# Four-layer graph attention on one core: the third step becomes a one-head step, and the small columns W·a of layers 1 to 3 are built by TensorE

## The chip, the core and the metric

The kernel runs on one core of one Trainium2 chip. The engines named below are TensorE (PE, with its weight loads as PEld), VectorE (DVE), ScalarE (ACT), GpSimd (POOL) and SyncE (SP), which issues nearly all DMAs. The metric is device time of one execution in microseconds. All arithmetic is float32, and the masks are stored as bytes.

## The reference

Sixteen graphs of 1024 nodes with 256 features pass through four graph-attention layers that share one adjacency matrix. Layers 0 and 2 have four heads of 64 features, layers 1 and 3 one head of 256. Each layer normalises its input, projects it, forms attention weights from two inner products per node and head, takes a masked softmax over the neighbours, aggregates, applies an activation and adds the result to x. Cut to what is computed:

```python
h = jnp.maximum(_layernorm(x, axis=-1), 0.0)
q = (h @ W).reshape(B, N, H, D)
e_src = jnp.einsum('bnhd,d->bnh', q, a_src)
e_dst = jnp.einsum('bnhd,d->bnh', q, a_dst)
e = e_src[:, :, None, :] + e_dst[:, None, :, :]
e = jnp.where(e >= 0, e, ALPHA * e)
e = jnp.where(mask, e, NEG_INF)
attn = jax.nn.softmax(e, axis=2)
x = x + jax.nn.elu(jnp.einsum('bijh,bjhd->bihd', attn, q))   # relu in layer 3
```

## The kernel before, in words

One step is one layer of one graph: 64 steps, numbered from 0. Four graphs are in flight at a time (`STREAMS`), and `order_of_steps` (L699) interleaves them. With H for a four-head step and 1 for a one-head step, the order starts H H H 1 H 1 1 H 1 H 1 and alternates from there on. Step 0 is graph 0 in layer 0, step 1 graph 1 in layer 0, step 2 graph 2 in layer 0, step 3 graph 0 in layer 1, step 4 graph 3 in layer 0, steps 5 and 6 graphs 1 and 2 in layer 1, step 7 graph 0 in layer 2.

**The weights.** A softmax weight is, up to a factor that cancels, max(G, r)·mask, where G is one row broadcast to all 128 partitions and r a column. For each head there are eight tiles w of 128 x 1024 (L411), one DVE instruction each. A four-head step thus has 32 tiles, a one-head step 8. The tiles live in a pool "w" of 18 slots (`WBUFS`). The pool also takes the small tensors of `weight_columns`. A slot is free again when the last reader of its tile has run.

**The aggregation.** A step has eight groups of matmuls (L428), each closed by an ACT copy of the result y (L443). In a four-head step two groups use the eight tiles of one head. A group goes through its four row blocks one after another, and each block needs all eight tiles, so only the first quarter of a group can run while the last tile is being made. In a one-head step each group is one row block of all eight tiles.

**The preparation of a step** (`preparation`, L231) has 21 pieces: statistics of x on DVE (L243), their combination (L263 to L284, mostly on POOL), normalisation on ACT (L290), the transpose of both halves of the rows, projection on PE (L332) with ACT copies (L334), the column factors (L340 to L351), and the row G. In most steps the transpose is done by two ACT copies and one DMA (L299, L301, L307), and the row G by a PE transpose, a write to DRAM and a read that broadcasts it (L358, L362, L386), which ACT copies into PSUM (L397). Steps 0 and 1 and the last step transpose on PE (L321). Steps 0 and 63 also build their G on PE (L394).

**The end of a step** (`finish`, L449) divides by the softmax sums, applies the activation and adds to x. It is shared between DVE, POOL and ACT. The third step from the end has a form of its own (L504 to L533) in which DVE does nearly all of it, since the last step needs its result at once.

**The order.** It is written out by hand, and each engine runs its instructions in program order. Position 8n + k is group k of step n. Each piece of the preparation of step n has a due position, from one of the tuples `FOUR`, `ONE`, `SOON` and so on, plus a start. At each position the loop (L673 to L694) emits in this order: end pieces of the step before that are due before the group, the tiles that the group needs, the group, further end pieces, row copies G, a piece of `later` (below), due preparation, and then tiles in advance, at most 18 beyond the last head that is done. A step's tiles can be emitted only after its last preparation piece.

**W·a.** Two columns per head of the weights are W·a, so that the projection yields the inner products too. `weight_columns` (L136) computes them by layer in four pieces: fetch a as one row (one DMA, L145), spread it over the partitions by a matmul and an ACT copy (L152, L155), eight DVE operations and a square (L162, L163, L169), and a bound for the exponents (L175 to L182). For layers 1, 2 and 3 the dictionary `later` puts these pieces at positions p, p + 1, p + 2 and p + 8 with p = 1, 27 and 43.

Of the kernel before, what the change touches and what calls it, by code (L numbers as in the profile page):

```python
# [26 lines left out]
F32 = mybir.dt.float32  # L27
# [20 lines left out]

FOUR = (-8, -8, -5, 0, 1, 0, 3, 5, 5, 5, 5, 1, 4, 5, 5, 5, 5, 6, 8, 8, 10)
SHORT = (-4, -4, -4, 0, 1, 0, 3, 5, 5, 5, 5, 1, 4, 5, 5, 5, 5, 6, 8, 8, 10)
NEXT = (-4, -4, -4, 1, 3, 2, 5, 8, 8, 8, 8, 4, 7, 8, 8, 8, 8, 9, 10, 10, 12)
ONE = (2, 2, 2, 3, 4, 3, 5, 7, 7, 7, 7, 4, 7, 8, 8, 8, 8, 8, 11, 11, 12)
SOON = (0, 0, 0, 1, 2, 1, 3, 4, 4, 5, 5, 2, 5, 6, 6, 7, 7, 7, 8, 8, 10)
FIRST = (-4, -4, -4, -2, -0.9, -1, -1, -0.8, -0.8, -0.8, -0.8, 0, 0, 1, 1, 1, 1, 1, 2, 2, 4)
TIGHT = (4, 4, 4, 5, 6, 5, 7, 8, 8, 8, 8, 6, 8, 9, 9, 9, 9, 9, 10, 10, 12)
LAST = (0, 0, 0, 1, 3, 2.8, 2.8, 4, 4, 4, 4, 4, 4, 4, 4, 4, 4, 4, 5, 5, 5)
LATE = (0, 0, 0, 1, 2, 1, 3, 4, 4, 4, 4, 2, 4, 5, 5, 5, 5, 5, 6, 6, 8)

# [10 lines left out]
def kernel(ctx: ExitStack, tc: tile.TileContext, x, adj, ws, avs, out):  # L71
# [41 lines left out]
    xs = {}  # L113
    state = [dict() for _ in steps]

    def bank(*shape):
        t = ps.tile([P, 512], F32, name="bank")
        n = math.prod(shape)
        if len(shape) == 1:
            return t[:, 0:n]  # L120
        names = "abc"[:len(shape)]
        return t[:, 0:n].rearrange(f"p ({' '.join(names)}) -> p {' '.join(names)}",
                                   **dict(zip(names, shape)))
# [10 lines left out]
                            in_=ws[l][k * P:(k + 1) * P, :].rearrange("p (h d) -> p h d", h=H))  # L134

    def weight_columns(l):  # L136

        H, slope, hs, _ = LAYERS[l]
        D = F // H
        st = {}  # L140

        def vectors(queue=nc.sync):

            st["a"] = work.tile([P, HALF, H, D], F32, name="w", bufs=WBUFS)
            queue.dma_start(  # L145
                out=st["a"][0:1, 2:4],
                in_=bass.AP(tensor=avs[l].tensor, offset=avs[l].offset,
                            ap=[[0, 1], [D, 2], [hs, H], [1, D]]))

        def spread():  # L150
            pa = bank(2, H, D)
            nc.tensor.matmul(pa.rearrange("p t h d -> p (t h d)"), lhsT=ones[0:1, :],  # L152
                             rhs=st["a"][0:1, 2:4].rearrange("p t h d -> p (t h d)"),
                             start=True, stop=True)
            nc.scalar.activation(st["a"][:, 0:2], pa, AF.Copy)  # L155

        def columns(ks=range(K)):
            for k in ks:
                for part in range(2):
                    prod = st["a"][:, 2 + part]  # L160
                    wk = heads_of(wx[l], H)[:, k]
                    nc.vector.tensor_mul(prod, wk[:, :, 0:D], st["a"][:, part])  # L162
                    nc.vector.tensor_reduce(  # L163
                        wk[:, :, D] if part else wx[l][:, k, F + H:F + 2 * H], prod, AX.X, ALU.add)
            if K - 1 not in ks:
                return
            st["sq"] = small.tile([P, K, H], F32, name="sq", bufs=1)
            wd = heads_of(wx[l], H)[:, :, :, D]
            nc.vector.tensor_tensor(st["sq"], wd, wd, op=ALU.mult)  # L169

        def bound():

            pn = bank(H)
            for k in range(K):
                nc.tensor.matmul(pn, lhsT=ones, rhs=st["sq"][:, k, :], start=(k == 0),  # L175
                                 stop=(k == K - 1))
            top = small.tile([P, 1], F32, name="top", bufs=1)
            nc.vector.tensor_reduce(top, pn, AX.X, ALU.max)
            nc.gpsimd.tensor_tensor(top, top, half1, op=ALU.pow)
            nc.gpsimd.tensor_scalar(cbias[l], top, 16.01, None, op0=ALU.mult)  # L180
            nc.gpsimd.tensor_scalar(nbias[l], top, -16.01 * slope, None, op0=ALU.mult)
            nc.gpsimd.tensor_scalar(rbias[l], top, -16.01 * (1.0 - slope), SHIFT,  # L182
                                    op0=ALU.mult, op1=ALU.add)

        return vectors, spread, columns, bound

    pairs = {}
# [43 lines left out]
    def preparation(n):  # L231
# [6 lines left out]
        def stats(half):  # L238
            if half == 0:
                st["bn"] = small.tile([P, C, 6], F32, name="bn")  # L240
            bn = st["bn"]
            for c in range(half * HALF, (half + 1) * HALF):
                nc.vector.bn_stats(bn[:, c, :], xs[b][:, c, :])  # L243
            q = slice(half * HALF, (half + 1) * HALF)
            if n == len(steps) - 1:
                combine(q, nc.vector)
            elif n == 0:
                if half == 1:
                    combine_end(slice(0, HALF), nc.vector)
                combine(q, nc.vector)  # L250
            elif H == 1:

                combine(q, nc.gpsimd)
                combine_end(q, nc.gpsimd)
# [55 lines left out]
                st["turned", half].rearrange("p s n i -> p (n i) s"), AF.Copy)  # L310

        def transpose(half, k):
            if 1 < n < len(steps) - 1:

                (merge if k else split)(half)
                return
            if k == 0:
                st["hT", half] = prep.tile([P, K, HALF * P], F32, name="rows", bufs=HBUFS)
            pt = bank(HALF, P)
            for q in range(HALF):  # L320
                nc.tensor.transpose(pt[:, q, :], st["xn", half][:, k, q, :], ident)  # L321
            nc.scalar.activation(st["hT", half][:, k, :], pt.rearrange("p q i -> p (q i)"),
                                 AF.Copy)
# [28 lines left out]

        def rows():

            if n == len(steps) - 1:
# [12 lines left out]


        out += [factors, rows, lambda: fetch_heads(n + 1), lambda: None]  # L370
        if n == len(steps) - 1:
            st["stats"], st["combined"] = stats, lambda half: combine_end(
                slice(half * HALF, (half + 1) * HALF), nc.vector)
            out[0:3] = [lambda: None] * 3
        return [(at, piece) for at, piece in zip(agenda_of[n], out, strict=True)]

    def direct(n, h):

        return h == 0 and n in (0, len(steps) - 1)

    def fetch(n, h):

# [16 lines left out]
    def weights(n, h, jc):  # L399


        parts = 2 if n == len(steps) - 1 else 1
        if parts > 1 and jc:
            return
        js = range(C) if parts > 1 else (jc,)
# [43 lines left out]
    def finish(n):  # L449
# [51 lines left out]
            if half == 1 and b + STREAMS < B:  # L501
                load(b + STREAMS)

        if n == len(steps) - 3:  # L504

            def early(half):
                xh, yh, r = views(half)
                rb = r[:, :, None].to_broadcast([P, HALF * H, D])
                e = st["e", half] = prep.tile([P, HALF * H, D], F32, name="rows", bufs=HBUFS)
                nc.vector.scalar_tensor_tensor(e, yh, 0.0, rb, op0=ALU.min, op1=ALU.mult)  # L510
                if half == 0:
                    exponential(half)
                nc.vector.tensor_tensor(yh, yh, rb, op=ALU.mult)

            def late(half):
                xh, yh, r = views(half)
                e = st["e", half]
                nc.vector.scalar_tensor_tensor(e, e, -1.0, yh, op0=ALU.add, op1=ALU.max)
                nc.vector.tensor_add(xh, xh, e)

            def begin():
                divide()
                early(0)
                late(0)
                state[-1]["stats"](0)
                early(1)
                state[-1]["combined"](0)

            def end():
                late(1)  # L530
                state[-1]["stats"](1)
                state[-1]["combined"](1)

            return [(-1, begin), (1, lambda: exponential(1)), (1, end)]


        at = (0, 0, 0, 0, 1, 1, 1) if slack(n) and H > 1 else (0, 0, 1, 1, 2, 2, 3)
# [63 lines left out]
    for n, (b, l) in enumerate(steps):  # L601
# [4 lines left out]
            free = 8 * over + (8 if l == 0 else 2 if LAYERS[steps[over][1]][0] == 1 else 4)  # L606
        last[b % STREAMS] = n
        start = 8 * (n - 2)
        kind = ONE if LAYERS[l][0] == 1 else SOON if n < 3 else FOUR
        if kind is FOUR and free > start + kind[0]:  # L610
            kind = SHORT if slack(n - 2) else NEXT
        if kind is ONE and free > start + kind[0]:
# [4 lines left out]
        if n == len(steps) - 1:  # L617
            kind, start = LAST, 8 * (n - 1)
        agenda_of.append([start + k for k in kind] if n > 1 else FIRST)
        if n > 2:  # L620

# [77 lines left out]
def order_of_steps(B, L):  # L699
# [3 lines left out]

    depth = B // STREAMS * L
    one = [[(k // L * STREAMS + s, k % L) for k in range(depth)] for s in range(STREAMS)]
    turns = [0, 1, 2, 0, 3, 1, 2] + [0, 3, 1, 0, 2, 1, 3, 2] * (depth // 2 - 1) + [3]
    return [one[s].pop(0) for s in turns]


# [22 lines left out]
```

## Time and profile before

| | us |
|---|---|
| median of 3 runs | 2451.44 |
| lowest and highest run | 2450.72, 2453.48 |
| the profiled execution's own time | 2451.16 |
| its span, first to last instruction | 2449.4 |
| first group of matmuls L428 starts | 45.77 |
| step 7 starts (its first group L428) | 335.93 |

The profile is of one execution; its span is 1.8 us shorter than that execution's time. Lines such as L428 are those of the kernel printed above. A row of a timeline gives the start, the duration, the engine, the line, the operation and how many instructions were merged into it. Matmuls of float32 count as two instructions each, so a group of a four-head step has 128 and a group of a one-head step 16. Some records of matmuls can be missing.

### The profile page before, as it was taken

To read this page: it belongs to the slowest core of one execution; us is meant where nothing else is said; L and a number is where in the kernel's file an instruction comes from. 1 tells how busy PE (TensorE), PEld (TensorE's weight loads), DVE (VectorE), ACT (ScalarE), POOL (GpSimd) and SP (SyncE) were. 2 spreads that over 40 slices of the span, in tenths; PEclk is the share of its full clock that TensorE was granted. 3 is DMA by queue.
4 is the path that set the end of the run, shared out by engine and by line. 5 is a ranking of instruction groups with operands and counts; after the bars stand their busy time and mean duration, and the time that the engine had idled before them with its cause. 6 is when DMAs were issued, how large, how long until landed. Compare 5 with 4: busy or idle time off the path is not lost.

```text
span 2449.4 us, 86561 instructions
## 1 busy us (share of the span) xinstructions
PE 2393.3 (98%) x39127; PEld 2149.5 (88%) x39127; DVE 2048.9 (84%) x2168; ACT 1478.8 (60%) x2499; POOL 1069.9 (44%) x1346
## 2 busy tenths in 40 slices
PE   7999999999999999999999999999999999999999
PEld 5888788889898899898898888899988988888897
DVE  8988688988888988888988888888888888888794
ACT  5465676556665656765656765666665567656542
POOL 3345455543345454544333554543443445544331
PEclk9999999999999999999999999999999999999999
DMA  4322232233333322333433323223323323323320
GB/s 181 81 54 62 44 79 62 71 103 91 97 77 90 80 63 46 79 71 96 114 92 85 79 62 71 71 54 97 97 80 105 97 46 79 71 62 77 73 54 35
DMA packets 290442, 191.84 MB, mean 78 GB/s; under 512 B 259998, under 2 KB 262806, under 8 KB 288152
## 3 DMA queue, kind: packets, MB, share of 16 engines
q1 hardware_dynamic: 290062, 186.29, 30.0%
q8 instruction: 307, 5.03, 0.8%
q14 instruction: 63, 0.52, 0.1%
q10 hardware_dynamic: 10, 0.00, 0.0%
HBM read 104.87 MB, written 17.43 MB: 50 GB/s over the span
## 4 chain that ended last, share of the span: by engine, by line
PE 80%; ACT 7%; DVE 6%; DMA 5%; issue 2%; POOL 0%; SPq 0%; DVEq 0%; ACTq 0%
PE bank L428 62%; PE bank L332 17%; DVE w L411 4%; DMA gs<-grow 2%; ACT rows L290 2%; DMA grow<-gT 2%; ACT rows L299 1%; ACT g L397 1%; ACT rows L481 1%; DVE bn L243 1%; ACT y L443 1%; ACT rows L307 0%; DMA rows<-rows 0%; DVE rows L487 0%; PE bank L358 0%
## 5 line engine op out<-in xcount | busy, mean ns | idle before, releaser
L428 PE MATMUL bank<-whx,w 128*64 128x65 f32 x36864 | 1896.7, 240 | 18.7 <-DVE w L411 9.8
L428 PEld LDWEIGHTS bank<-whx,w 128*64 128x64 f32 x36864 | 1745.6, 144 | 176.2 <-issue 21.7
L411 DVE SCALAR_TENSOR_TENSOR w<-g,rcol,mask 128x1024 f32<-128x1024 f32 (+1 forms) x1288 | 1539.8, 1268 | 195.9 <-PE bank L428 161.1
L344 POOL TENSOR_TENSOR whx<-whx 128x1024 f32<-128x1024 f32 x128 | 244.6, 1911 | 845.8 <-ACT whx L342 845.8
L443 ACT ACTIVATE y<-bank 128x260 f32<-128x260 f32 (+1 forms) x504 | 191.9, 381 | 560.3 <-PE bank L428 560.2
L332 PE MATMUL bank<-wx,rows 128*128 128x264 f32 (+1 forms) x2048 | 485.8, 391 | 14.7 <-ACT y L443 8.8
L332 PEld LDWEIGHTS bank<-wx,rows 128*128 128x128 f32 x2048 | 381.5, 191 | 90.3 <-ACT y L443 14.8
L475 POOL TENSOR_TENSOR y<-y,r 128x1024 f32<-128x1024 f32 x124 | 257.6, 2086 | 224.6 <-DVE rows L474 188.8
L334 ACT ACTIVATE whx<-bank 128x264 f32<-128x264 f32 (+1 forms) x512 | 194.1, 388 | 190.6 <-PE bank L332 190.3
L290 ACT ACTIVATE rows<-x,shift,rstd 128x256 f32<-128x256 f32 x512 | 264.5, 588 | 66.6 <-POOL shift L284 61.4
L488 POOL TENSOR_TENSOR x<-x,rows 128x1024 f32<-128x1024 f32 x94 | 222.3, 2365 | 178.4 <-DVE rows L487 178.4
L307 ACT ACTIVATE rows<-rows 128x2048 uint16<-128x2048 uint16 x122 | 261.7, 2145 | 20.6 <-DMA rows<-rows 20.6
L299 ACT ACTIVATE rows<-rows 128x2048 uint16<-128x2048 uint16 x122 | 233.1, 1911 | 3.9
L487 DVE SCALAR_TENSOR_TENSOR rows<-rows,y 128x1024 f32<-128x1024 f32 x94 | 186.0, 1979 | 45.2 <-ACT rows L481 39.7
L243 DVE BATCH_NORM_STATS2 bn<-x 128x6 f32<-128x256 f32 x512 | 175.7, 410 | 34.3 <-POOL x L488 31.1
L397 ACT ACTIVATE g<-gs 128x1024 f32<-128x1024 f32 x158 | 161.7, 1023 | 66.7 <-DMA gs<-grow 54.0
L278 POOL TENSOR_TENSOR rstd<-rstd,neghalf 128x4 f32<-128x4 f32 (+1 forms) x97 | 121.2, 1249 | 41.0 <-DVE shift L279 33.8
L481 ACT ACTIVATE rows<-rows 128x1024 f32<-128x1024 f32 x96 | 100.6, 1048 | 9.9 <-DVE rows L510 7.9
L464 DVE RECIPROCAL r<-y 128x32 f32<-128x32 f32 (+1 forms) x63 | 17.3, 275 | 98.5 <-ACT y L443 98.5
L474 DVE SCALAR_TENSOR_TENSOR rows<-y,r 128x1024 f32<-128x1024 f32 x58 | 68.5, 1222 | 1.1
L342 ACT ACTIVATE whx<-whx,nbias 128x16 f32<-128x16 f32 (+1 forms) x128 | 40.2, 314 | 4.2
L340 ACT ACTIVATE rcol<-whx,rbias 128x16 f32<-128x16 f32 (+1 forms) x128 | 39.9, 312 | 4.2
(73 smaller groups left out, 463.7 us busy)
## 6 DMA issues: line engine op xcount, KB each, us to landing
gs<-grow SPq DMA_DIRECT2D x158, 512.0 KB
x<-in_x SPq DMA_DIRECT2D x15, 1024.0 KB
out<-x SPq DMA_DIRECT2D x30, 512.0 KB
w<-in_adj SPq DMA_DIRECT2D x8, 512.0 KB
rows<-rows SPq DMA_TRANSPOSE x122
x<-in_x SPq DMA_DIRECT2D x2, 512.0 KB
wx<-in_L_gnn_W SPq DMA_DIRECT2D x8, 128.0 KB
out<-x SPq DMA_DIRECT2D x8, 128.0 KB
```

Of the source, the lines that this page charges most:

```text
L243: nc.vector.bn_stats(bn[:, c, :], xs[b][:, c, :])
L290: nc.scalar.activation(xn[:, :, q, :], xs[b][:, c, :].rearrange("p (k i) -> p k i", k=K), AF.Relu, bias=st["shift"][:, c:c + 1], scale=st[ ...
L299: nc.scalar.activation(bits, xn.rearrange("p (n s) -> p s n", s=2), AF.Copy)
L307: nc.scalar.activation(st["hT", half].rearrange("p k i -> p (k i)").bitcast(U16).rearrange("p (n s) -> p n s", s=2), st["turned", half].re ...
L332: nc.tensor.matmul(pw, lhsT=st["hT", half][:, k, q * P:(q + 1) * P], rhs=wx[l][:, k, :], start=(k == 0), stop=(k == K - 1))
L334: nc.scalar.activation(st["whx"][:, c, :], pw, AF.Copy)
L344: nc.gpsimd.tensor_tensor(wh[:, :, :, 0:D], wh[:, :, :, 0:D], wh[:, :, :, D:D + 1].to_broadcast([P, HALF, H, D]), op=ALU.mult)
L411: nc.vector.scalar_tensor_tensor(state[n]["w", h, j][:, s], state[n]["g", h][:, s], state[n]["rcol"][:, j, h:h + 1], masks[LAYERS[steps[n] ...
L428: nc.tensor.matmul(acc[o % P:o % P + cols, q, :], lhsT=st["w", h, jc][:, o:o + cols], rhs=st["whx"][:, jc, h * (D + 1):(h + 1) * (D + 1)], ...
L443: nc.scalar.activation(st["y"][:, i0:i0 + per, h, :], acc, AF.Copy)
L475: nc.gpsimd.tensor_tensor(yh, yh, rb, op=ALU.mult)
L488: nc.gpsimd.tensor_add(xh, xh, e)
```

## The change

The order of steps becomes H H 1 H 1 H 1 H 1 and so on: step 2 is graph 0 in layer 1, step 3 graph 2 in layer 0, step 4 graph 1 in layer 1, step 5 graph 3 in layer 0. Steps 6 and later are what they were. A tuple `rush` holds step 2 and the last step. What held for the last step alone now holds for both: statistics combined on DVE, PE transposes in place of the DMA, G of the only head by PE, tiles made in two halves of 512 columns. Step 0 ends in the form that the third step from the end had, except that the multiplication by 1/sum stays on POOL. Steps 2 and 3 get due positions of their own. For layers 1 to 3, a goes down the partitions by one-element-wide DMAs, W is transposed by matmuls with the identity, and W·a comes from four matmuls, two ACT copies and one POOL square. Layer 0 keeps the old form.

```diff
-SOON = (0, 0, 0, 1, 2, 1, 3, 4, 4, 5, 5, 2, 5, 6, 6, 7, 7, 7, 8, 8, 10)
+THIRD = (1, 1, 2, 2, 3, 2.8, 2.8, 2.9, 2.9, 2.9, 2.9, 4, 4, 4, 4, 4, 4, 4, 5, 5, 5)
+FOURTH = (-2, -2, -2, 6, 7, 6, 8, 9, 9, 9, 9, 7, 9, 10, 10, 10, 10, 10, 10, 10, 12)
...
+    rush = (2, len(steps) - 1)
...
+        def vectors_down():
+            a = st["a"] = work.tile([P, K, 2 * H], F32, name="w", bufs=WBUFS)
+            if H > 1:
+                nc.gpsimd.memset(a, 0.0)
+            for part, column in ((1, 0), (0, H)):
+                for h in range(H):
+                    for k in range(K):
+                        if h * D // P <= k <= ((h + 1) * D - 1) // P:
+                            lo = max(h * D, k * P)
+                            size = min((h + 1) * D, (k + 1) * P) - lo
+                            nc.sync.dma_start(
+                                out=a[lo - k * P:lo - k * P + size, k, column + h:column + h + 1],
+                                in_=bass.AP(tensor=avs[l].tensor,
+                                            offset=avs[l].offset + h * hs + part * D + lo - h * D,
+                                            ap=[[1, size], [1, 1]]))
+        def turned():
+            pt = bank(K, K, P)
+            for k in range(K):
+                wk = heads_of(wx[l], H)[:, k, :, 0:D]
+                size = min(D, P)
+                for lo in range(0, F, size):
+                    h, d = divmod(lo, D)
+                    nc.tensor.matmul(pt[lo % P:lo % P + size, lo // P, k, :],
+                                     lhsT=wk[:, h, d:d + size], rhs=ident, start=True, stop=True)
+            st["wT"] = work.tile([P, K, K, P], F32, name="w", bufs=WBUFS)
+            nc.scalar.activation(st["wT"], pt, AF.Copy)
+        def products():
+            pw = bank(K, 2 * H)
+            for k in range(K):
+                for d in range(K):
+                    nc.tensor.matmul(pw[:, k, :], lhsT=st["wT"][:, d, k, :], rhs=st["a"][:, d, :],
+                                     start=(d == 0), stop=(d == K - 1))
+            wd = heads_of(wx[l], H)[:, :, :, D]
+            nc.scalar.activation(wd, pw[:, :, 0:H], AF.Copy)
+            nc.scalar.activation(wx[l][:, :, F + H:F + 2 * H], pw[:, :, H:2 * H], AF.Copy)
+            st["sq"] = small.tile([P, K, H], F32, name="sq", bufs=1)
+            nc.gpsimd.tensor_tensor(st["sq"], wd, wd, op=ALU.mult)
+        if l > 0:
+            return vectors_down, turned, products, bound
         return vectors, spread, columns, bound
...
-        if n == len(steps) - 3:
+        if n + 2 in rush:
+            after = state[n + 2]
             def early(half):
...
                 nc.vector.scalar_tensor_tensor(e, yh, 0.0, rb, op0=ALU.min, op1=ALU.mult)
-                if half == 0:
-                    exponential(half)
-                nc.vector.tensor_tensor(yh, yh, rb, op=ALU.mult)
+                (nc.vector if n else nc.gpsimd).tensor_tensor(yh, yh, rb, op=ALU.mult)
...
             def begin():
                 divide()
                 early(0)
+            def middle():
+                exponential(0)
                 late(0)
-                state[-1]["stats"](0)
+                after["stats"](0)
                 early(1)
-                state[-1]["combined"](0)
+                after["combined"](0)
             def end():
+                exponential(1)
                 late(1)
-                state[-1]["stats"](1)
-                state[-1]["combined"](1)
-            return [(-1, begin), (1, lambda: exponential(1)), (1, end)]
+                after["stats"](1)
+                after["combined"](1)
+            return [(-1, begin), (-1 if n else 1, middle), (1 if n else 2, end)]
...
-        kind = ONE if LAYERS[l][0] == 1 else SOON if n < 3 else FOUR
+        kind = ONE if LAYERS[l][0] == 1 else FOUR
...
-        if n == len(steps) - 1:
-            kind, start = LAST, 8 * (n - 1)
+        if n == 3:
+            kind, start = FOURTH, 8
+        if n in rush:
+            kind, start = THIRD if n == 2 else LAST, 8 * (n - 1)
...
-    turns = [0, 1, 2, 0, 3, 1, 2] + [0, 3, 1, 0, 2, 1, 3, 2] * (depth // 2 - 1) + [3]
+    turns = [0, 1, 0, 2, 1, 3, 2] + [0, 3, 1, 0, 2, 1, 3, 2] * (depth // 2 - 1) + [3]
```

The other lines of the diff replace `n == len(steps) - 1` by `n in rush` in `stats`, `transpose`, `rows`, `direct`, `weights` and at the end of `preparation`.

More of the change, by code (lines that the diff above doesn't have):

```diff
@@ L312, in transpose @@
         def transpose(half, k):
-            if 1 < n < len(steps) - 1:
+            if n > 1 and n not in rush:
                 (merge if k else split)(half)
@@ L353, in rows @@
         def rows():
-            if n == len(steps) - 1:
+            if n in rush:
                 return
@@ L370, in preparation @@
         out += [factors, rows, lambda: fetch_heads(n + 1), lambda: None]
-        if n == len(steps) - 1:
+        if n in rush:
             st["stats"], st["combined"] = stats, lambda half: combine_end(
@@ L377, in direct @@
     def direct(n, h):
-        return h == 0 and n in (0, len(steps) - 1)
+        return h == 0 and (n == 0 or n in rush)
     def fetch(n, h):
@@ L399, in weights @@
     def weights(n, h, jc):
-        parts = 2 if n == len(steps) - 1 else 1
+        parts = 2 if n in rush else 1
         if parts > 1 and jc:
@@ L616 @@
             start = max(free, agenda_of[-1][0] + 5, start - LATE[7])
-        if n == len(steps) - 1:
-            kind, start = LAST, 8 * (n - 1)
+        if n == 3:
+            kind, start = FOURTH, 8
+        if n in rush:
+            kind, start = THIRD if n == 2 else LAST, 8 * (n - 1)
         agenda_of.append([start + k for k in kind] if n > 1 else FIRST)
```

## The prediction

> **What bounds the kernel now.** I read the page's busy times first, then a table by stage (0, the first group at 45.77, the end of step 2's first group at 139.40, the start of step 7 at 335.93, the end), then the timelines of DVE, PE and POOL in the second and third stage, then the groups of instructions for prices.
>
> ```profile
> PE 2393.3 (98%) x39127; PEld 2149.5 (88%) x39127; DVE 2048.9 (84%) x2168; ACT 1478.8 (60%) x2499; POOL 1069.9 (44%) x1346
> ```
> ```profile
> 45.77:139.40 93.63, 84.69 (x2241) 78.09 (x2240) 93.46 (x105) 47.25 (x80) 32.08 (x54) 0.96 0.31 73
> 139.40:335.93 196.53, 188.32 (x2497) 166.36 (x2497) 151.00 (x170) 120.86 (x202) 98.48 (x124) 0.98 0.26 60
> 335.93:2449.40 2113.47, 2090.34 (x34240) 1883.01 (x34239) 1769.67 (x1827) 1283.11 (x2166) 925.53 (x1140) 1.00 0.31 77
> ```
>
> Columns: stretch, its length, busy PE, PEld, DVE, ACT, POOL, then granted PE clock, DMA share, GB/s. From 335.93 on PE is busy 98.9% and the change leaves those steps alone, so only the 290 us between 45.77 and 335.93 are at stake. In them PE idles 93.63 - 84.69 = 8.9 us and 196.53 - 188.32 = 8.2 us. In the first stretch DVE never rests (93.46 of 93.63): it is the bound. In the second it is PE.
>
> ```profile
> 73.47 26.30 DVE L411 SCALAR_TENSOR_TENSOR w<-g,rcol,mask 128x1024 f32<-128x1024 f32 x22
> 99.69 0.34 DVE L464 RECIPROCAL r<-y 128x32 f32<-128x32 f32 x1
> 124.09 10.10 PE L428 MATMUL bank<-whx,w 128*64 128x65 f32 x252 [0.71 <-DVE w L411]
> 136.24 3.14 PE L428 MATMUL bank<-whx,w 128*64 128x65 f32 x100 [0.85 <-DVE w L411]
> 140.50 3.75 PE L332 MATMUL bank<-wx,rows 128*128 128x258 f32 x16 [1.12 <-ACT rows L307]
> ```
> ```profile
> 236.91 2.70 DVE L243 BATCH_NORM_STATS2 bn<-x 128x6 f32<-128x256 f32 x8
> 241.91 1.22 DVE L487 SCALAR_TENSOR_TENSOR rows<-rows,y 128x1024 f32<-128x1024 f32 x1
> 250.40 9.10 PE L428 MATMUL bank<-whx,w 128*64 128x65 f32 x228 [0.71 <-DVE w L411]
> ```
> ```profile
> L321 PE MATMUL bank<-ident,rows 128*128 128x128 f32 x48 | 10.4, 337 | 7.4 <-ACT rows L290 7.3
> L162 DVE TENSOR_TENSOR w<-wx,w 128x256 f32<-128x256 f32 x16 | 7.9, 496 | 0.0
> L163 DVE TENSOR_REDUCE wx<-w 128x1 f32<-128x256 f32 x8 | 3.4, 420 | 0.3
> L519 DVE TENSOR_TENSOR x<-x,rows 128x1024 f32<-128x1024 f32 x2 | 2.5, 1225 | 0.1
> L518 DVE SCALAR_TENSOR_TENSOR rows<-rows,y 128x1024 f32<-128x1024 f32 x2 | 2.4, 1223 | 0.1
> ```
>
> Read: tiles come every 26.30 / 22 = 1.195 us, 9.6 a head, while a head's two groups take PE 7.8 (a group is 3.9; 3.5 in a one-head step). After a head's last tile three quarters of its first group still follow (136.24, 3.14). At 124 and 250 PE waits tile by tile, and afterwards its groups run slow: 252 instructions at 3.9/128 us are 7.7, not 10.1; 228 are 7.0, not 9.1. That is 2.4 and 2.1 us lost.
>
> [...] granted clock 0.83 in 120 to 140, though the gaps recorded there are under 1 us. [...] L487 takes 1.22 alone and 2.86 beside POOL L475 at 189. [...] No a of this kind is in the trace; its nearest, the row a of layer 3, landed 1.7 us after its issue at 283.62.
>
> **The change, part by part.**
>
> *W·a of layer 1, positions 1 to 3.* DVE loses 4 x 0.42 + 4 x 0.42 + 0.16, in the trace 70.13 to 73.47: 3.4 us. PE swaps 1.1 (L152) for eight instructions of 128 columns and eight tiny ones, some 1.45 us by L332's 0.11 per 128 columns; here it is not the bound. But the slots tell against it: when tile 24 is wanted, tiles 8 to 23, a and the new wT hold all 18, so DVE waits for the end of group 3 of step 0 (67.5 in the trace, which nothing before it moves). Without step 2's statistics (2.65) DVE would be there at 36.53 + 9.63 + 16 x 1.195 = 65.2. The wait is 2.3 us.
>
> *DVE up to the end of step 1's tiles.* 67.5 + 24 x 1.195 + 2.65 (statistics of step 3) = 98.9 for tile 48, against 99.7 before. Then 1/sum and the first activation 1.45, two tiles 2.4: 102.7. Middle: L518, L519 forms 1.15 + 1.2, four statistics 1.36, seven small combinations 1.0, activation 1.15, two more 0.35: 6.2, so 109.0. Six tiles: 116.2. End: 1.15 + 1.2 + 1.36 + 1.0, a wait for POOL's power of 1.1, 0.35: 6.2, so 122.4. Eight tiles: 132.0. Before, step 1's last tile came at 124.0; the 8 us are the end of step 0, mostly done by POOL before, and the combination.
>
> *PE in step 1.* Step 2's second half is normalised after 122.4 (four ACT pieces of 0.52, PE behind each): transposed 125.0, copied 126.2, projected (3.7) 129.9, then group 5 133.8, G by eight transposes (1.0, L394 at 31.37) 134.8, groups 6 and 7 142.6. The first half hides in PE's wait for tiles before 116.2. The floor without this chain is DVE's 132.0 + 3.1 + 3.9 = 139.0. Before, the same point, with one group more done by 139.40, is 135.5. Stage: +7.1, at the floor +3.5. Step 2's tiles (16 halves, 0.66 each) come in time: eight by 140.1.
>
> *From there to step 7.* Both orders have the same groups and projections left. Before: 200.4 us, of which 8.2 idle and 2.1 slow clock, so 190.1 of work. PE adds layers 2 and 3: 2 x (1.45 - 1.1) = 0.7, so 190.8. What is idle:
> - Step 3's first half is turned by a DMA and merged by ACT at about 151, PE arrives at 149.8: 1.0 (0.5 to 3).
> - Layer 2's products at position 29. POOL clears a behind the last add of step 2, and that stands behind DVE's second L487, due after tile 25 of step 3. With u the end of group 1: tiles 18 to 23 need its slots, u + 7.2; L487, two tiles, L487, u + 12; POOL add 2.4 and clearing, u + 14.7. SP then issues eight DMAs (0.3 to 0.6 each by L145 and L386), landing at u + 18.4 to u + 21.5, while PE is ready at u + 17.6 (four groups and 0.9 plus). SP's queue holds step 4's row behind them (L362, L386); ACT waits for it at its copy G before freeing banks, which can add 1 or 2. Wait 0.8 to 4.6; I take the middle, 2.7. Before, PE waited 2.0 for the rows a of layers 2 and 3.
> - DVE in step 3 has no statistics to take and no columns, so the starvation at 246 goes. Other waits 1.0 (0 to 2); layer 3 has no clearing and none counted.
>
> Stage: 190.8 + 4.7 = 195.5, a gain of 4.9.
>
> *The end of the kernel.* The third step from the end issues the same instructions, the ACT exponential one DVE instruction later in the program on another engine: nothing, or at worst 1.2 us on DVE if ACT's wait took in the later one; DVE is not the last there.
>
> **Sum.** +7.1 - 4.9 = +2.2 us against the profiled execution, 2451.16 to 2453.4; with the median 0.3 above it, 2453.7. About 0.2%, 4.9 us, is what a measurement of this kernel can tell from no change.
>
> **Rivals.**
> 1. *Faster: alternation pays in full.* The 17.1 idle and 4.5 slow-clock us are the price of three four-head steps in a row. If step 1 ends at DVE's floor (+3.5), the slot wait costs nothing (-2.3) and step 3 and layer 2 wait 1.3 together (190.8 + 1.3 - 200.4 = -8.3), it is -7: about 2444; half way, 2446. For it: DVE has only 10.6 us of tiles in step 2. Against: PE's chain in step 1 is in program order.
> 2. *Slower: layer 2's a.* SP at 0.6 us or more a DMA and ACT's wait for the row behind it make the stop at position 29 some 8 us instead of 2.7: +7.5, 2459. It decides from a stop of 5.4 us on. For it: the chain crosses four engines in order. Against: DVE may reach L487 earlier.
> 3. *The clock.* PE has nothing from 105.9 (end of group 3) to 110.4 in step 1[...]. The first half's projection then runs slow, mostly hidden[...].
>
> **How the numbers follow.** Forecast with rival 3: within 0.2%, 0.43. Rival 1: 0.27. Rival 2, or the bounds of step 1's chain and step 3 adding to it: 0.30. The sum's own bounds are -7 and +9; the range 2444 to 2461 takes them in. Of its own the forecast has 2447 to 2456.
>
> **What would show it.** Step 2's first 257-column group starts near 142.6, later than 139; DVE's 1/sum of step 0 near 99; a pause of DVE near 65 until 67.5; PE idle of a few us before the products in step 3; no tile-by-tile waits after 145; step 7's first group near 338. If step 2 starts at 139 or before, or step 7 before 333, the chain in step 1 was mis-sized and it is faster. If POOL clears a early, rival 2 falls.

## The result and the profile after

| | before | after |
|---|---|---|
| median, us | 2451.82 (4 runs) | 2470.43 (4 runs) |
| lowest, highest | 2450.72, 2453.48 | 2470.04, 2473.04 |
| the profiled execution's own time | 2451.16 | 2473.04 |

The ratio is 1.0077, 95% interval 1.0061 to 1.0094: 18.6 us slower, outside the predicted range of 2444 to 2461. The profiled execution of the kernel after is its slowest, 2.6 us above its median, so the stages below add up to 21.9 us. From the preparation of a step on, a line of the kernel after stands 48 lines below its like in the printed kernel: L476 is L428, the groups; L380 is L332, the projection; L459 is L411, the tiles; L445 is L397, ACT's copy of a row G; L331 and L332 are L283 and L284, the end of the combination. The offset is 46 in a_old_wa and 43 in the two runs whose names begin with b. L201, L214 and L223 are new: the fetch of a, the turning of W and the products.

The page's line of busy times, of the kernel after:

```profile
PE 2402.5 (97%) x39200; PEld 2161.7 (87%) x39200; DVE 2054.4 (83%) x2173; ACT 1471.9 (60%) x2503; POOL 1057.5 (43%) x1326
```

PE's busy time grew by 9.2 us, with 73 instructions more and stretches at a slower clock (0.93 granted in the first stage, 0.96 in that stage before); the rest of the loss is idle time. The table by stage of the kernel after says where (stretch, length, busy PE, PEld, DVE, ACT, POOL, granted clock, DMA share, GB/s). Its stretches are: first group to the start of step 2; to the start of step 7; to the end.

```profile
44.54:146.00 101.46, 88.47 (x2151) 80.67 (x2151) 94.10 (x111) 33.95 (x73) 19.30 (x23) 0.93 0.11 29
146.00:351.45 205.45, 194.07 (x2662) 172.95 (x2661) 157.89 (x171) 128.27 (x215) 98.52 (x135) 0.98 0.30 69
351.45:2471.30 2119.85, 2091.08 (x34240) 1886.93 (x34239) 1768.09 (x1825) 1282.42 (x2166) 925.82 (x1140) 1.00 0.31 77
```

The same stretches of the kernel before are 45.77 to 135.50, to 335.93, to the end: 89.73, 200.43 and 2113.47 us. So the first stage cost 11.7 us more, the second 5.0 more instead of less, and the third, whose work is the same, 6.4 more; the first group starts 1.2 earlier.

**First stage.** Timeline of the kernel after, DVE, then POOL, then PE:

```profile
65.46 19.16 DVE L459 SCALAR_TENSOR_TENSOR w<-g,rcol,mask 128x1024 f32<-128x1024 f32 x16 [1.05 <-PE bank L476]
...
96.68 0.34 DVE L512 RECIPROCAL r<-y 128x32 f32<-128x32 f32 x1
...
107.70 1.86 DVE L331 TENSOR_TENSOR shift<-shift,rstd 128x4 f32<-128x4 f32 x1 [0.92 <-POOL rstd L326]
...
123.02 1.85 DVE L331 TENSOR_TENSOR shift<-shift,rstd 128x4 f32<-128x4 f32 x1 [1.08 <-POOL rstd L326]
...
107.64 1.90 POOL L560 TENSOR_TENSOR y<-y,r 128x1024 f32<-128x1024 f32 x1
...
122.96 1.89 POOL L392 TENSOR_TENSOR whx<-whx 128x1024 f32<-128x1024 f32 x1
...
110.51 2.80 PE L369 MATMUL bank<-ident,rows 128*128 128x128 f32 x8 [5.36 <-ACT rows L338]
113.14 5.68 PE L380 MATMUL bank<-wx,rows 128*128 128x258 f32 x16
...
128.46 4.86 PE L380 MATMUL bank<-wx,rows 128*128 128x258 f32 x16
...
138.16 14.83 PE L476 MATMUL bank<-whx,w 128*64 128x65 f32 x288
```

And DVE in the last step, which combines its statistics by the same line:

```profile
2417.86 0.17 DVE L331 TENSOR_TENSOR shift<-shift,rstd 128x4 f32<-128x4 f32 x1 [1.04 <-POOL rstd L326]
```

The pause for slots is 1.05 us, and 1/sum starts at 96.68, earlier than forecast. Then the time goes. L331 multiplies two tensors of 128 x 4. In the last step, where POOL has no product beside it, it takes 0.17. Here it takes 1.86 and 1.85, and both times it ends within 0.03 us of a POOL instruction of 1.9 that began 0.06 ahead of it (107.64 + 1.90 and 107.70 + 1.86; 122.96 + 1.89 and 123.02 + 1.85). So the cost to this tiny instruction was the whole POOL instruction; what held it, the trace does not show. On PE the two projections take 5.68 and 4.86 where 3.75 is usual; the granted clock was 0.65 from 113.1 to 118.8 and 0.77 from 128.4 to 133.4. The last line holds the last two groups of step 1 (256 instructions, 7.8 us), so step 2 starts at 146.0.

**Second stage.** Timeline of the kernel after, ACT, DVE and PE, around the rows G of step 3:

```profile
177.72 1.91 ACT L347 ACTIVATE rows<-rows 128x2048 uint16<-128x2048 uint16 x1
179.53 1.01 ACT L445 ACTIVATE g<-gs 128x1024 f32<-128x1024 f32 x1
...
190.24 1.03 ACT L445 ACTIVATE g<-gs 128x1024 f32<-128x1024 f32 x1 [5.59 <-DVE w L459]
191.20 1.19 ACT L382 ACTIVATE whx<-bank 128x258 f32<-128x258 f32 x4
...
180.58 14.39 DVE L459 SCALAR_TENSOR_TENSOR w<-g,rcol,mask 128x1024 f32<-128x1024 f32 x12 [16.12 <-ACT g L445]
...
191.66 5.53 PE L476 MATMUL bank<-whx,w 128*64 128x65 f32 x128 [3.95 <-issue]
```

DVE stood still for 16.12 us until step 3's first row G was copied. SP issued the read of that row at 169.82, but from 171.44 to 179.6 ACT normalises and splits the rows of step 4, which its program has first. ACT then meets the third row G, which waits 5.59 for DVE to finish with a PSUM place; step 4's copies L382 are queued behind it, so PE finds no free bank and stands for 3.95. The profile names nothing that ended this stop ("issue"), so the bank is inferred: the first of the four copies ends 0.1 before PE starts again. A free bank alone would not have spared the whole stop, since DVE's eighth tile, which every row block of the group needs, is done only at 190.2; both come from the late row G. The group after that stop takes 5.53 instead of 3.95.

Timeline of the kernel after, POOL, SP and PE, at layer 2's products:

```profile
216.01 2.39 POOL L536 TENSOR_TENSOR x<-x,rows 128x1024 f32<-128x1024 f32 x1 [1.17 <-DVE rows L535]
218.33 0.11 POOL L194 MEMSET w<- 128x16 f32 x1
...
218.47 5.02 SPq L201 DMA_DIRECT2D w<-in_L_gnn_a  x8
...
224.38 0.36 PE L223 MATMUL bank<-w 128*128 128x8 f32 x2 [3.46 <-DMA grow<-gT]
225.32 0.81 PE L223 MATMUL bank<-w 128*128 128x8 f32 x6 [0.58 <-DMA w<-in_L_gnn_a]
225.98 3.55 PE L380 MATMUL bank<-wx,rows 128*128 128x264 f32 x8
230.23 5.61 PE L380 MATMUL bank<-wx,rows 128*128 128x264 f32 x24 [0.70 <-ACT y L491]
```

The chain of rival 2 is there link by link: the add, the clearing, eight DMAs in 5.02 us, PE waiting. (The profile puts the 3.46 down to another DMA, grow; the experiment a_early_a below settles it.) The stop is 3.46 + 0.58 + 0.70 = 4.7, and the eight projection instructions after it take 3.55 where 24 take 5.61, so 1.7 too long.

**Third stage.** What PE waited for from step 7 on, first in the kernel before, then in the kernel after (total, times, longest):

```profile
PE bank L428 <- issue: 7.4, 13, 1.2
PE bank L332 <- issue: 0.6, 2, 0.4
```
```profile
PE bank L476 <- issue: 12.2, 13, 2.8
PE bank L380 <- issue: 2.1, 2, 1.6
```

14.3 us against 8.0, so 6.3 more. The other waits came to 10.0 for 10.9, and PE's busy time in this stage grew by 0.7: these stops make up nearly all of the 6.4. Timeline of the kernel after, SP and PE, at the longest of them:

```profile
596.52 0.34 SPq L434 DMA_DIRECT2D gs<-grow  x1
596.91 0.89 SPq L546 DMA_DIRECT2D out<-x  x2
...
593.27 3.95 PE L476 MATMUL bank<-whx,w 128*64 128x65 f32 x127
598.01 3.95 PE L476 MATMUL bank<-whx,w 128*64 128x65 f32 x128 [0.79 <-issue]
604.77 0.27 PE L476 MATMUL bank<-whx,w 128*64 128x65 f32 x1 [2.81 <-issue]
604.97 9.07 PE L380 MATMUL bank<-wx,rows 128*128 128x264 f32 x32
```

These two stops and the slow projection after them (9.07 where 7.39 is usual) are 5.3 us by themselves. They are exactly 128 products apart, which with their weight loads are 256 instructions. The page's part on DMA queues has this line:

```profile
q8 instruction: 307, 5.03, 0.8%
```

That is 307 packets and 5.03 MB of instructions: 16.4 KB a packet, and 5.03 MB over 2 x 39200 PE instructions is 64 bytes each, so by this estimate a packet is 256 of them. That the queue is PE's is inferred from this count and from the times. One of its packets began at 602.6, 0.6 us into the stop of 2.81, and took 0.95; PE went on 1.2 us after its end. All 15 stops that the profile puts down to issue in this stage end 1.2 to 1.5 us after the end of such a packet. The DMA engines were busy 0.87 and more of each us from 599.6 to 602.6, and 0.08 of the next.

### The profile page after: what moved, and what is told of

Its sections match the earlier page's. It is cut to its first block, busy times and chain, and to the rows that moved or that the text cites. A ratio compares the mean times of both kernels' runs of the same rounds, so it can differ in the third digit from the quotient of the medians.

```text
span 2471.3 us, 86718 instructions
## 1 busy us (share of the span) xinstructions
PE 2402.5 (97%) x39200; PEld 2161.7 (87%) x39200; DVE 2054.4 (83%) x2173; ACT 1471.9 (60%) x2503; POOL 1057.5 (43%) x1326
## 3 DMA queue, kind: packets, MB, share of 16 engines
q8 instruction: 307, 5.03, 0.8%
## 4 chain that ended last, share of the span: by engine, by line
PE 85%; ACT 5%; DMA 4%; DVE 3%; issue 2%; SPq 0%; POOL 0%; DVEq 0%; ACTq 0%
PE bank L476 67%; PE bank L380 18%; DMA gs<-grow 2%; DMA grow<-gT 2%; ACT rows L338 1%; DVE w L459 1%; ACT rows L347 1%; ACT g L445 1%; ACT rows L529 1%; ACT y L491 0%; DVE bn L291 0%; ACT rows L355 0%; PE bank L406 0%; DMA rows<-rows 0%; DVE mask L264 0%
## 5 line engine op out<-in xcount | busy, mean ns | idle before, releaser
L476 PE MATMUL bank<-whx,w 128*64 128x65 f32 x36864 | 1893.8, 241 | 20.3 <-issue 16.5
L476 PEld LDWEIGHTS bank<-whx,w 128*64 128x64 f32 x36864 | 1745.7, 144 | 173.3 <-issue 30.1
L459 DVE SCALAR_TENSOR_TENSOR w<-g,rcol,mask 128x1024 f32<-128x1024 f32 (+1 forms) x1296 | 1540.7, 1261 | 213.1 <-PE bank L476 165.2
L380 PE MATMUL bank<-wx,rows 128*128 128x264 f32 (+1 forms) x2048 | 490.6, 394 | 13.3 <-ACT y L491 9.0
L380 PEld LDWEIGHTS bank<-wx,rows 128*128 128x128 f32 x2048 | 385.9, 193 | 90.4 <-ACT y L491 15.3
L382 ACT ACTIVATE whx<-bank 128x264 f32<-128x264 f32 (+1 forms) x512 | 193.3, 387 | 195.0 <-PE bank L380 194.9
L355 ACT ACTIVATE rows<-rows 128x2048 uint16<-128x2048 uint16 x120 | 257.3, 2144 | 18.4 <-DMA rows<-rows 18.1
L347 ACT ACTIVATE rows<-rows 128x2048 uint16<-128x2048 uint16 x120 | 229.3, 1911 | 3.8
L445 ACT ACTIVATE g<-gs 128x1024 f32<-128x1024 f32 x157 | 160.7, 1024 | 73.4 <-DMA gs<-grow 64.3
```

What stands on the lines that cost most here:

```text
L347: nc.scalar.activation(bits, xn.rearrange("p (n s) -> p s n", s=2), AF.Copy)
L355: nc.scalar.activation(st["hT", half].rearrange("p k i -> p (k i)").bitcast(U16).rearrange("p (n s) -> p n s", s=2), st["turned", half].re ...
L380: nc.tensor.matmul(pw, lhsT=st["hT", half][:, k, q * P:(q + 1) * P], rhs=wx[l][:, k, :], start=(k == 0), stop=(k == K - 1))
L382: nc.scalar.activation(st["whx"][:, c, :], pw, AF.Copy)
L445: nc.scalar.activation(g, state[n]["gs", h], AF.Copy)
L459: nc.vector.scalar_tensor_tensor(state[n]["w", h, j][:, s], state[n]["g", h][:, s], state[n]["rcol"][:, j, h:h + 1], masks[LAYERS[steps[n] ...
```

## The experiments

All were timed in five rounds beside the kernel before. "To step 7" is from the first group to step 7's first group in the run's profile; the kernel before has 290.2, the kernel after 306.9. Each such figure is of one execution.

| run | median us | ratio to before, 95% interval | to step 7, us |
|---|---|---|---|
| a_old_wa | 2466.09 | 1.0080 (1.0065 to 1.0094) | 306.3 |
| b_new_wa | 2451.49 | 1.0016 (1.0009 to 1.0023) | 294.8 |
| a_early_a | 2463.34 | 1.0061 (1.0049 to 1.0073) | 301.2 |
| a_g_first | 2464.31 | 1.0069 (1.0056 to 1.0083) | 302.5 |
| a_shift_pool | 2464.68 | 1.0067 (1.0049 to 1.0086) | 300.6 |
| a_stats_late | 2466.52 | 1.0076 (1.0058 to 1.0094) | 304.0 |
| a_four | 2451.25 | 1.0009 (0.9996 to 1.0022) | 288.5 |
| b_new_wa_early | 2443.58 | 0.9978 (0.9969 to 0.9988) | 287.0 |
| a_four_32 | 2447.11 | 0.9994 (0.9984 to 1.0004) | 288.7 |
| a_four_64 | 2454.22 | 1.0016 (1.0008 to 1.0024) | 292.3 |
| after_64 | 2481.03 | 1.0120 (1.0103 to 1.0137) | 314.4 |

**Which part of the change.** Theory C: the loss is several chains of waits, each of a few us. Rival W: the columns by TensorE are the loss. Rival O: the order is. The first run takes the columns out of the kernel after, the second puts them alone into the kernel before.

```diff
-        if l > 0:
-            return vectors_down, turned, products, bound
         return vectors, spread, columns, bound
```

> The changed kernel with one part undone: the columns W a of layers 1 to 3 are built by DVE again, the order of steps and the rush of step 2 stay. Theory C (several chains, each a few us): the stop of 4.7 us before the products of layer 2 and the slow clock after it (some 1.7 us) go, PE's wait for the row a comes back (about 1 us), and layer 1's eight DVE operations come back (3.4 us) but take the place of a wait for a slot of 1 us. Net 3 to 5 us faster than the changed kernel: 2465 to 2468. Rival W (the columns by TensorE are the whole loss): 2452 or so. Rival O (the order is the whole loss, the columns by TensorE even help): 2472 or more.

> The kernel before with one part of the change alone: columns W a of layers 1 to 3 by TensorE, order of steps as before. Theory C: DVE saves 3.4 us in the stretch to 140 us, where it is the bound, less a wait for slots of about 2; in layer 2 the columns leave DVE just before PE starves at 246, and the clearing of a has no long chain before it as step 3 is a one-head step: 1 to 6 us faster than before, 2446 to 2451. Rival W: about 2470. Rival O: 2446 to 2452.

W falls: without the columns the order alone still costs 0.80%. Both numbers of theory C missed as well: a_old_wa is no faster than the kernel after, where C had 3 to 5 us less, and b_new_wa is 0.16% slower than the kernel before, where C had it 1 to 6 us faster. So far O fits best; whether the order's cost is a set of waits that can be removed is what the next runs ask. In a_old_wa the stop at layer 2 shrinks to 1.49, but a group of 5.53 instead of 3.95 follows it, and DVE's 3.3 us of column work come back in the first stage: about as much is spent as was saved. PE's stop before step 4's first group is there too, here in the timeline of a_old_wa:

```profile
194.20 5.53 PE L474 MATMUL bank<-whx,w 128*64 128x65 f32 x128 [3.96 <-issue]
```

The columns alone do take 3.3 us out of the first stage (step 3's projection starts at 137.22, not at 140.50) and give back more at layer 2, in the timeline of b_new_wa:

```profile
208.07 0.56 PE L218 MATMUL bank<-w 128*128 128x8 f32 x2 [4.74 <-DMA w<-in_L_gnn_a]
209.26 1.42 PE L218 MATMUL bank<-w 128*128 128x8 f32 x6 [0.62 <-DMA w<-in_L_gnn_a]
210.53 9.14 PE L471 MATMUL bank<-whx,w 128*128 128x257 f32 x32
```

The two groups after the stop take 9.14 where 7.2 is usual.

**One wait at a time, in the kernel after.** First layer 2's fetch and clearing seven positions earlier:

```diff
-            for i, piece in zip((0, 1, 2, 8), layer[l]):
+            for i, piece in zip((-7 if l == 2 else 0, 1, 2, 8), layer[l]):
```

> The changed kernel, with one edit: the clearing and fetch of a for layer 2 stand seven positions earlier, at position 20 in step 2, so that they stand ahead of POOL's add of step 3 and of the row of step 4. Theory C: the stop before the products (3.46 + 0.58 + 0.70 us) and about 1.7 us of slow clock after it go: 2464 to 2466. If the stop is only in place of a wait that comes anyway: no change, 2470.

To step 7 it is 5.7 us shorter: the stop and its slow projection go (6.4 by the lines above), and PE's stop before step 4's group grows from 3.95 to 4.50.

Then step 3's last piece of preparation one position earlier, so that ACT copies its row G ahead of step 4's rows:

```diff
-FOURTH = (-2, -2, -2, 6, 7, 6, 8, 9, 9, 9, 9, 7, 9, 10, 10, 10, 10, 10, 10, 10, 12)
+FOURTH = (-2, -2, -2, 6, 7, 6, 8, 9, 9, 9, 9, 7, 9, 10, 10, 10, 10, 10, 10, 10, 11)
```

> The changed kernel, with one edit: step 3 counts as prepared one position earlier (19 in place of 20), so that ACT copies its first row G ahead of the normalisation and the split of step 4's second half. Theory C: DVE starts step 3's tiles some 4 us earlier, PE's pause of 3.95 us at 187.7 and 1.6 us of slow clock after it go: 2465 to 2467. If DVE's late start costs nothing because PE would wait for ACT's copies of the projection anyway: 2470.

4.4 us shorter; the stop of 3.95 is gone, in the timeline of a_g_first:

```profile
188.37 1.14 PE L380 MATMUL bank<-wx,rows 128*128 128x258 f32 x4 [0.61 <-ACT y L491]
189.44 3.95 PE L476 MATMUL bank<-whx,w 128*64 128x65 f32 x128
```

Then the last two instructions of step 2's combination, L331 and L332, on POOL and ahead of its long product:

```diff
-                slice(half * HALF, (half + 1) * HALF), nc.vector)
+                slice(half * HALF, (half + 1) * HALF), nc.vector if n > 2 else nc.gpsimd)
...
                 after["stats"](0)
+                if n == 0:
+                    after["combined"](0)
                 early(1)
-                after["combined"](0)
+                if n:
+                    after["combined"](0)
```

> The changed kernel, with one edit: for step 2 the last two small combinations (shift times rstd, times -0.5) are done by POOL right after its power, ahead of its product for the second half, in place of DVE. In the changed kernel the first of them takes DVE 1.85 us twice in place of 0.15, each time beside a POOL product of 1.9 us. Theory C (DVE's chain in step 1 sets when PE may begin step 2[...]): 3.4 us plus two waits of 1 us leave DVE's chain, step 2 starts 2 to 4 us earlier, total 2 to 4 us less than the changed kernel, so 15 to 17 us above before. If PE's own order is the limit in step 1, or the 1.85 us are only a longer record: no change, 19 above before.

6.3 us shorter. POOL takes 0.20 for what held DVE 1.86, here the timeline of POOL in a_shift_pool, and DVE goes from 1/sum to the end of the eighth tile after the second combination in 31.8 us instead of 37.9. The edit removes the hold and DVE's two waits for POOL (0.92 and 1.08) together and does not tell them apart.

```profile
109.43 0.20 POOL L331 TENSOR_TENSOR shift<-shift,rstd 128x4 f32<-128x4 f32 x1
...
121.78 0.20 POOL L331 TENSOR_TENSOR shift<-shift,rstd 128x4 f32<-128x4 f32 x1
```

Last, step 3's statistics after step 2's combination instead of before it:

```diff
-FOURTH = (-2, -2, -2, 6, 7, 6, 8, 9, 9, 9, 9, 7, 9, 10, 10, 10, 10, 10, 10, 10, 12)
+FOURTH = (4, 4, 4, 6, 7, 6, 8, 9, 9, 9, 9, 7, 9, 10, 10, 10, 10, 10, 10, 10, 12)
```

> The changed kernel, with one edit: the statistics of step 3 (eight instructions, 2.65 us on DVE) move from position 6 to position 12, behind the last tile of step 1, where DVE waits 3.7 us for G. Theory C: whatever DVE saves before the end of step 0 comes out at the start of step 2 one for one, 2 to 2.7 us less than the changed kernel, 16 to 17 above before. If PE's chain in step 1 has slack against DVE: no change, 19 above before.

Step 2 starts 2.8 us earlier after the first group, and step 7 2.9; the median shows nothing that the interval could tell from the kernel after. For each of these four alone the interval of the time overlaps that of the kernel after; the profile tells them apart, the median doesn't.

**All four together.**

> The changed kernel with four edits together: layer 2's a seven positions earlier, step 3 prepared at position 19, step 2's last combinations on POOL, step 3's statistics at position 12. Theory C: the savings add up, 4 + 2 to 4 + 3 + 2.5: 12 us less than the changed kernel, 6 to 8 above before. Rival O (the order itself costs, since DVE has to end step 0 alone and the work of PE is the same): it stays at least 5 above before. If the waits mask one another: 10 to 14 above.

Here the time decides: 1.0009, its interval clear of the kernel after. Singly they shortened the way to step 7 by 5.7 + 4.4 + 6.3 + 2.9 = 19.3 us, together by 18.4: they add up, as theory C says, and by more than the 12 us that it expected. Rival O's "at least 5 above before" falls too: it is 2.8. What is left is a kernel 1.7 us shorter than before up to step 7 and no faster in all.

**The columns in the old order, with the earlier fetch.**

> The kernel before, its order of steps kept, with columns W a of layers 1 to 3 by TensorE and layer 2's a cleared and fetched seven positions earlier (position 20). With the fetch at 27 this was 3.7 us above before, with a stop of 4.74 + 0.62 us before the products and about 2 us of slow clock after it, while step 3's projection came 3.6 us earlier. Theory C: the stop goes, 2 to 4 us below before. If the fetch was not what held the products: 4 above before.

No stop is left, in the timeline of b_new_wa_early:

```profile
203.56 1.04 PE L218 MATMUL bank<-w 128*128 128x8 f32 x8
204.46 7.20 PE L471 MATMUL bank<-whx,w 128*128 128x257 f32 x32
```

At 0.9978 it beats both kernels. Moving one fetch turned the columns from a loss of 0.16% into a gain of 0.22%, the intervals far apart. It also shows where a_four stands: a_four has the same columns and the same fetch, in the new order with that order's other repairs, yet it takes 1.5 us longer to step 7 (288.5 for 287.0) and its interval lies above (from 0.9996, against up to 0.9988). So the 1.7 us that a_four wins to step 7 come from the columns; no run here shows a gain from the order.

**The third stage.** Do its stops come from the place of an instruction in its block of 256? More turns of a mask tile, early, where PE stood idle, move every later instruction by 64 or 128 places (N is 32 or 64):

```diff
-            for jc in range(C):
+            for jc in [*range(C), *([0] * (N if c == C - 1 else 0))]:
                 nc.tensor.transpose(pm[:, jc, :], sgn[:, jc, :], identb)
```

> The four repairs, and 32 of the mask's 128x128 turns issued once more in the turn of the last mask tile, where TensorE stood idle 3.7 us: nothing left out, 32 weight loads and 32 products more (2.1 us, beside other waits). Question: from step 7 on, after waits 14.3 us in TensorE stops that are put down to issue, before only 8.0, a_four 12.4; in step 13 two such stops are exactly 128 products apart. Theory F (the stops are TensorE waiting for its next 16.4 KB of instructions, 256 of them, whose fetch stands behind the 512 KB fetches and stores just issued): in step 13 the stops lie after about 94 and 222 products from the row group's end, not after 126 and 254, the stop of 2.8 us shrinks or goes, and the sum of issue stops after step 7 changes by 2 us or more; median 2445 to 2452. Rival P (the stops come from how VectorE and ScalarE stand to TensorE): stops stay after 126 and 254, the sum within 1 us of 12.4, median 2451 to 2452.5.

> The same with 64 turns more (4.3 us, 0.6 of them beyond the idle stretch), half a block of instructions. F: stops of step 13 after about 62 and 190 products, the sum of issue stops changes, median 2445 to 2453. P: stops after 126 and 254, sum within 1 us of 12.4, median 2451.5 to 2453.

> The changed kernel, no repair, with the same 64 turns more. F: in step 13 the stops lie after about 64 and 192 products, not after 127 and 255; if the changed kernel's extra stops from step 7 on (14.3 us against 8.0) are a matter of where its blocks of instructions end, their sum falls to 8 to 11 and the median by 2 to 6 us, to 2460 to 2464. P: sum 13 to 15, median 2465 to 2468 on this chip's scale (after stood at 1.0077 times before).

Rival P, that the stops come from how VectorE and ScalarE stand to TensorE, falls: it had them stay in step 13, and in none of the three is one left there. F, that PE waits for its next block of instructions, had the stop of 2.8 shrink or go, which it did, but it also had stops after 94 and 222 products (62 and 190, 64 and 192), and none came there. In the timeline of a_four_32 the same 256 products run through:

```profile
576.71 7.69 PE L476 MATMUL bank<-whx,w 128*64 128x65 f32 x256
```

Stops came up at other steps instead, in a_four_64 and after_64 again in pairs some 128 products apart; here one right after a fetch of a row G and two stores, SP and PE in the timeline of after_64:

```profile
680.24 0.34 SPq L434 DMA_DIRECT2D gs<-grow  x1
680.63 0.89 SPq L546 DMA_DIRECT2D out<-x  x2
...
681.85 3.95 PE L476 MATMUL bank<-whx,w 128*64 128x65 f32 x128 [0.91 <-issue]
688.06 0.45 PE L476 MATMUL bank<-whx,w 128*64 128x65 f32 x8 [2.26 <-issue]
688.44 9.07 PE L380 MATMUL bank<-wx,rows 128*128 128x264 f32 x32
```

The runs hold a further test of F. Six kernels have the same PE instructions in the same order around step 13 (after, a_early_a, a_g_first, a_shift_pool, a_stats_late, a_four), while the time that they take to step 7 differs by up to 18 us. In all six the pair stands at the same two products of step 13, within one. So the stops are bound to places in PE's stream of instructions and are no accident of one execution.

Their sum is less steady: in these six it is 11.2 to 14.3 us from step 7 on. In a_four_32 it is 4.6 for a_four's 12.4, clear of that spread (its profiled execution is near its fastest); 9.9 in a_four_64 lies just below it and 13.5 in after_64 (for 14.3) within it, and the intervals of the times of a_four and a_four_32 overlap. So F is right that the place decides, and its hope for after_64 was wrong: a shift moves the stops, and their sum need not fall. Which transfers a boundary meets may decide that; no run tests it. after_64 lost 7.5 us more before step 7: its turns delayed the last mask tile, for which DVE waited 2.44 us, PE then waited for step 0's tiles, and DVE's wait for slots grew from 1.05 to 3.44. "0.6 of them beyond the idle stretch" was mis-sized.

## Why the prediction was wrong

Against the profiled execution the forecast was +2.2 us and 21.9 came. The three stages missed by 3.4, 9.95 and 6.4.

*First stage, 142.6 forecast, 146.0 measured.* The wait for slots was 1.05, not 2.3, since the first group began 1.2 earlier and the slot came free 0.6 before that group ended; DVE's 1/sum came 2.2 before time. The step that failed is "DVE up to the end of step 1's tiles": from 1/sum to the end of the second combination I had 98.9 to 122.4, 23.5 us, and it took 96.68 to 125.08, 28.4. L331 is 3.4 of the 4.9, the uncounted wait for POOL's power in the first half 0.9. I had quoted the 1.22 of L487 that became 2.86 beside POOL, and then priced the small instructions as if POOL were idle. The trace before had a small one that was held: a product L162 of 128 x 256 at 295.34 took 1.70 beside POOL's L344, where its neighbours take 0.42. From there PE needed 20.9 for my 20.2, its second projection at a lower clock (4.86 for 3.7). a_shift_pool shows this step: with POOL's combination ahead of its product, 6.3 us go.

*Second stage, 195.5 forecast, 205.45 measured.* "Other waits 1.0" was the step that failed most. I counted for step 3 what DVE no longer has to do, and did not follow ACT's program order: step 3's row G lay behind step 4's rows, and that became PE's stop of 3.95 and 1.6 of slow clock, 5.5 us (a_g_first). "Layer 2's products", 2.7, was the right chain and too small: 4.7 and 1.7 of slow clock, 6.4 (a_early_a). PE also waited 1.75 for ScalarE's column of step 3 at 166.56. Against the forecast that is 5.5 + 3.7 + 1.75 - 1.0 = 9.95, the whole difference. It closes so well by luck, since smaller errors of the 190.8 us of work offset one another: the 8.2 of idle time were read from 139.40 on, while the stretch begins at 135.5 (9.0 from there), and the new columns cost PE 2.0 to 2.2 us a layer, not 1.45 (L214 1.16 and L223 1.05 in layer 3). The merge of step 3's rows took 0.93 of its 1.0, and the tile-by-tile waits after 146 did vanish, both as said.

*Third stage, 0 forecast, 6.4 measured.* "The change leaves those steps alone" is true of the work and not of where PE's stream of instructions is cut into packets of 16.4 KB. The stops there are 6.3 us more. That they are tied to places in the stream is shown; what makes one long and another short stays open.

*Rivals.* Rival 1 fell: even with its waits repaired the new order gains nothing (a_four). Its "half way, 2446" was also a slip: half way between 2444 and the forecast is 2449. Rival 2 had the right mechanism, and its stop stayed below its own 5.4, but the slow projection after it brings it to 6.4, not quite a third of the 21.9. Rival 3's clock is in the trace: after the gap of 5.36 the projection takes 5.68, and after 3.12 the next takes 4.86. I had taken it as "mostly hidden", which was my estimate; it was looked for at one place, and it follows each of the five stops of 2.8 us or more after the first group.

## What to carry to other kernels

When steps change places, read the program order of every engine between two steps that are now neighbours, ScalarE's copies above all: work that became cheaper on one engine may be worth nothing if its input now stands behind another step's (DVE stood 16.12 us here). Price small instructions of a chain by what runs beside them (1.86 us here beside a POOL product, 0.17 without), and add to a long stop of TensorE the slow work that follows it (1.1 to 1.9 us here after stops of 2.81 to 5.36). A new fetch goes where its buffer is cleared early: the same columns lost 0.16% or won 0.22% by its position alone.

## What the runs showed of the hardware

- DVE's L331, on two tensors of 128 x 4, took 1.86 and 1.85 us beside a POOL instruction of 1.9 and ended within 0.03 us of it; with no POOL product beside it the same line took 0.17.
- After a stop of 3.95 us PE's next work took 1.4 times as long as usual (5.53 for 3.95), and after one of 4.7 in three pieces, the longest 3.46, 1.9 times (3.55 for 1.87). The granted clock was 0.70 from 191.6 to 197.2 and from 224.3 to 230.0, and 1.00 from 197.2 to 212.0. Slow work followed shorter stops too: 3.12 us (4.86 for 3.75, clock 0.77), 2.81 (9.07 for 7.39, clock 0.81) and, in a_old_wa, 1.49 (5.53 for 3.95). It did not follow the five stops of 1.44 to 1.75 us in the kernel after: the granted clock was 1.00 right after each.
- PE stood for up to 2.8 us between instructions, where two stops followed each other 256 instructions apart. The instruction queue moved 16.4 KB a packet, by the estimate above 256 instructions, which fits the 128 products between stops, and the 15 stops of the third stage each ended 1.2 to 1.5 us after the end of a packet. Such stops summed to between 4.6 and 14.3 us of one execution. That the place in the stream decides where they stand is shown by the shifts and by the six kernels with the same stream. In the us before those 15 packets the DMA engines were busy 0.78 or more at 13, and at 63 of the other 253 packets of that stage. That the transfers just issued hold the fetch up was seen at the two places above and not tested by itself.
